# Order of the last attention group's softmax and of layer 2's first products, and of the loads of the later x groups, in a four-layer graph network kernel

## The chip, the cores and the metric

The kernel runs on one core of one Trainium2 chip. The metric is the device time of one execution in microseconds (us). The core has TensorE (PE, with its weight loads as PEld), VectorE (DVE), ScalarE (ACT), GpSimd (POOL) and SyncE (SP, which here only issues DMAs). Each works through its own queue of instructions in order, and they wait for each other by semaphores.

## The reference, cut to what matters

Four layers are applied to x (128 graphs, 64 nodes, 256 features, float32), each behind a layernorm and a relu and each added to x. The change touches the end of layer 1 and the start of layer 2.

```python
# layer 1: attention over the 64 nodes of a graph, 4 heads of 64
h = jnp.maximum(_layernorm(x), 0.0)
qkv = h @ W                                   # q, k, v
scores = einsum('bhid,bhjd->bhij', q, k) / sqrt(64) + mask   # mask: -inf where adj == 0
x = x + einsum('bhij,bhjd->bhid', softmax(scores), v)
# layer 2: mix over nodes, two linear layers with batchnorm
h = jnp.maximum(_layernorm(x), 0.0)
agg = einsum('nm,bmd->bnd', A_hat, h)
h = relu(batchnorm(agg @ W1.T + b1))          # fc1: 256 -> 512
x = x + batchnorm(h @ W2.T + b2)
```

Layer 0 (before) is a graph convolution followed by LSTMs over windows of nodes; layer 3 (after) is three graph convolutions.

## The kernel before

The 8192 tokens are cut into 16 groups of 512 (`NG = 16`), held as tiles `xs[0]` to `xs[15]` in SBUF. `NK = 4` groups make a quarter. The first four x tiles live from the start. The other twelve lie in memory that the LSTM stage has used; right after that stage one loop allocates them and issues all twelve loads (`load_x`, 512 KB each, on SP's queue).

Layer 1 is a loop over groups with a software pipeline. In iteration g, for group g: `values` (v = h times the weights, L779) in two halves, `queries_keys` (q and k by seven products of half-size blocks, L757, with ACT copies p at L171 and L172), `to_residual` (adds the LSTM's result to x four groups ahead, where there is one), `features` (the transposed h of the next group, ACT copies `hT` at L263, DVE differences at L196 to L200), and `softmax` (scores L803, mask L810, row maximum L817, subtraction L818, exp L819). For group g - 1: the row sums (`sums_of`, L824), `turn` (transposes of exp, L835, and copies eT), `attend` (exp times v, L848). For group g - 2: `add_output` (L860 on DVE divides by the row sums, L863 on POOL adds to x). The layernorm of group g + 2 (statistics L92 to L98 on DVE with a power on POOL, L96, and four ACT instructions, L111) stands after the subtraction.

Each half of `values` is copied from PSUM to one staging tile, `vt` (L784, a single buffer), and four DMAs on SP's queue (L787) regroup it into v. A next copy into `vt` waits until the four have landed.

Layer 2 begins inside the last iterations. `activated` is the layernorm and relu of a group, `mixed` its product with the adjacency (L143, copies at L155), `hidden` the products of fc1 (four of them, L729) and, for each, the batchnorm statistics (L735, DVE) and the bias on ACT (L736). In iteration 15 group 0 is mixed, group 1's layernorm is issued, then attend of group 14 and the scores and softmax of group 15. A seventeenth pass of the loop (g = 16) then does two products of group 0's fc1, group 1's mix, `add_output` of group 14, the turn of group 15, the other two products, attend of group 15 and its `add_output`. A loop over the groups 1 to 15 follows: layernorm and mix of group g + 1, all four products of group g.

The order in which the instructions stand on each engine is made by a scheduler from the program's order, its own estimates, and hints: `tc.issue_after(i)` lets nothing in its block stand ahead of instruction i. PSUM has eight banks, given out by `bank()`.

Of the kernel before, what the change touches and what calls it, by code (L numbers as in the profile page):

```python
# [8 lines left out]
F32 = mybir.dt.float32  # L9
# [29 lines left out]
def adj_preln_kernel(ctx: ExitStack, tc: tile.TileContext, x_in, adj, vec, bg0, bg1,  # L39
# [17 lines left out]
    def load_x(x, g):  # L57
        nc.sync.dma_start(out=x, in_=x_view[:, g * GT : (g + 1) * GT, :])
# [639 lines left out]
    xpool_b = ctx.enter_context(tc.tile_pool(name="xres_b", bufs=1, reuse_waits="tile"))  # L698
    for g in range(NK, NG):
        xs.append(xpool_b.tile([P, GT, D], F32, tag=f"x{g}", name=f"x{g}"))  # L700
        load_x(xs[g], g)


    def arena(pool):
# [14 lines left out]
    def mixed(g, copies):  # L719
        h = h1s[g][:, 0:2, :].rearrange("p a (b d) -> p (a b) d", d=D)  # L720
        return mix(h, ah2, 2, h1s[g][:, 2:4, :], copies)

    def hidden(g, w1, ms=range(4)):
        a = h1s[g]
        pss, counted = [], []
        for m in ms:
            ps = bank()
            for c in range(2):
                nc.tensor.matmul(  # L729
                    ps, lhsT=w1[:, c, m * P : (m + 1) * P], rhs=a[:, 2 + c, :],  # L730
                    start=(c == 0), stop=(c == 1),
                )
            pss.append(ps)
        for m, ps in zip(ms, pss):
            counted.append(nc.vector.bn_stats(st1[:, m, g, :], ps))  # L735
            nc.scalar.activation(  # L736
                a[:, m, :], ps, AF.Identity, bias=vecs[:, V_B1 + m : V_B1 + m + 1]
            )
        return counted


    with tc.tile_pool(name="att", bufs=2, reuse_waits="tile") as ap_:
# [28 lines left out]
        def values(hT, v, ks):  # L771


            for k in ks:
                ps = bank((P, 2, D))
                for t in range(2):
                    tok = (2 * k + t) * P
                    for c in range(2):
                        nc.tensor.matmul(  # L779
                            ps[:, t, :], lhsT=hT[:, c, tok : tok + P], rhs=wv[:, c, :],  # L780
                            start=(c == 0), stop=(c == 1),
                        )
                vt = ap_.tile([P, 2, D], F32, tag="vt", name="vt", bufs=1)
                nc.scalar.copy(vt, ps)  # L784
                for par in range(2):
                    for b in range(2):
                        nc.sync.dma_start(  # L787
                            out=v[par * 64 : par * 64 + 64, 4 * k + b : 4 * k + 4 : 2, :],
                            in_=vt[b * 64 : b * 64 + 64, :, par * P : (par + 1) * P],
                        )  # L790

        def softmax(qT, kT):


            e = ap_.tile([P, 2 * GT, 2, NODES], F32, tag="e", name="e")
            pss = [bank((P, 2 * GT, NODES)) for _ in range(2)]
            for t in range(GT):
                for m in range(2):
                    for b in range(2):
                        tok = t * P + b * NODES  # L800
                        for par in range(2):
                            rows = slice(par * 64, par * 64 + 64)
                            nc.tensor.matmul(  # L803
                                pss[par][b * 64 : b * 64 + 64, 2 * t + m, :],
                                lhsT=qT[rows, m, tok : tok + NODES],
                                rhs=kT[rows, m, tok : tok + NODES],
                                start=True, stop=True,
                            )
            for par in range(2):
                nc.vector.scalar_tensor_tensor(  # L810
                    e[:, :, par, :], pss[par], 0.125,
                    mask.unsqueeze(1).to_broadcast([P, 2 * GT, NODES]), ALU.mult, ALU.add,
                )
            ef = e.rearrange("p a q j -> p (a q) j")
            NH = 4 * GT
            mx = ap_.tile([P, NH, 1], F32, tag="mx", name="mx")
            nc.vector.tensor_reduce(mx[:, :, 0], ef, AX.X, ALU.max)  # L817
            sub = nc.vector.tensor_tensor(ef, ef, mx.to_broadcast([P, NH, NODES]), ALU.subtract)  # L818
            nc.scalar.activation(ef, ef, AF.Exp)  # L819
            ri = ap_.tile([P, 2 * GT, 2, 1], F32, tag="ri", name="ri")  # L820
            rif = ri.rearrange("p a q o -> p (a q o)")

            def sums_of():
                nc.vector.tensor_reduce(rif, ef, AX.X, ALU.add)  # L824
                nc.vector.reciprocal(rif, rif)

            return e, ri, sub.ins, sums_of

        def turn(e):

# [25 lines left out]
        def add_output(g, pss, ri):  # L856
            xv = xs[g].rearrange("p t (m q d) -> p (t m) q d", m=2, q=2)
            for par in range(2):
                o = ap_.tile([P, 2 * GT, NODES], F32, tag="o", name="o")
                nc.vector.tensor_tensor(  # L860
                    o, pss[par], ri[:, :, par, :].to_broadcast([P, 2 * GT, NODES]), ALU.mult
                )
                nc.gpsimd.tensor_tensor(out=xv[:, :, par, :], in0=xv[:, :, par, :], in1=o, op=ALU.add)  # L863

# [4 lines left out]
        nc.vector.tensor_tensor(wsum, wqk[0][1], ss[1], ALU.subtract)  # L871
        wqk_blocks = (*wqk, ss + [wdiff, wsum])
        last = None
        for g in range(NG + 1):
            if g == NG - NK + 1:
                hres_pool.__exit__(None, None, None)
                with tc.using_default_side("right"):
                    ar_right = ctx.enter_context(
                        tc.tile_pool(name="arena_r", bufs=NG // 2, reuse_waits="tile")
                    )  # L880
            if g == NG:

                hidden(0, w1, range(2))
                mixed(1, (on_scalar, on_scalar))
            if g < NG:
                hT_all, blocks = hT
                v = ap_.tile([P, 2 * GT, P], F32, tag="v", name="v")
                values(hT_all, v, (0,))
                q, k, finish = queries_keys(blocks)
                if g == 0:  # L890
                    h = normalized(1)
            if last is not None:
                with tc.issue_after(finish.behind):
                    if g > 1:
                        add_output(g - 2, pss, ri)
                    sums_of()
            if last is not None:
                e, ri, v_last = last
                eT, turned = turn(e)
            if g < NG:  # L900
                added = finish()
                if g == NG - 1:

                    w1 = w_att[:, :, 0:512]
                    w2 = w_att[:, :, 512:1024].rearrange("p a (b f) -> a p b f", f=D)
                    nc.sync.dma_start(out=w1, in_=w1t.rearrange("(c p) f -> p c f", p=P))
                values(hT_all, v, (1,))
            else:
                counted = hidden(0, w1, range(2, 4))
            if 0 < g <= NG - NK:  # L910
                to_residual(g + NK - 1, xs[g + NK - 1], ap_, 1)
            if g + 1 < NG:
                hT = features(transposed(h))
            if g == NG - 1:
                with tc.issue_after(mixed(0, (on_scalar, on_scalar))), tc.issue_after(added):
                    activated(ar_right, 1)
            if last is not None:
                pss = attend(eT, v_last)
            if g < NG:
                e, ri_next, sub, sums_of = softmax(q, k)  # L920
                last = (e, ri_next, v)
                with tc.issue_after(sub):
                    if g + 2 < NG:
                        h = normalized(g + 2)
                    elif g + 2 == NG:
                        activated(ar_right, 0)
            else:
                add_output(g - 1, pss, ri)
                after_attention = sub


    ar_left = ctx.enter_context(tc.tile_pool(name="arena_l", bufs=NG // 2 - 1, reuse_waits="tile"))
# [23 lines left out]

    behind = [[], [], counted]
    for g in range(1, NG):
        if g + 1 < NG:
            with tc.issue_after(behind[g - 1][-1].ins if behind[g - 1] else after_attention):  # L960
                pool = ar_right if g + 1 < NG // 2 else keep if g + 1 == NG // 2 else ar_left
                activated(pool, g + 1, (lambda: behind[g][1]) if behind[g] else None)
                mixed(g + 1, (on_scalar, on_vector))
        if g == 3:
            for a in range(2):
                nc.sync.dma_start(
                    out=w2[a], in_=w2t.rearrange("(a b p) f -> a p b f", a=2, p=P)[a]
                )
        behind.append(hidden(g, w1))
# [336 lines left out]
```

## Time and profile before

| | us |
|---|---|
| median of 3 runs (2499.6 to 2501.5) | 2500.47 |
| profiled execution, its own time | 2501.49 |
| its span | 2499.7 |
| PE busy / DVE busy / ACT busy / POOL busy | 2458.1 / 1514.5 / 1145.4 / 439.0 |
| mean granted PE clock | 0.993 |
| attention loop: mask of group 0 to the end of the last attend | 1232.3 to 1472.6 |

A line of the timeline gives the start in us from the span's start, the length in us, the engine, the line of the kernel, the operation, what it writes and reads, how many instructions are merged, and in brackets the engine's idle time ahead of it with what ended it. A line of the table of windows gives the stretch, the busy us of PE, PEld, DVE, ACT and POOL with the number of instructions, the mean granted PE clock (1.00 is full), the busy share of the DMA engines, and GB/s. A float32 matmul shows as two passes.

### The profile page before, as it was taken

The page shows a single profiled execution, that of the slowest core. Times are in us where ns is not written, and L with a number is a line of the kernel's source. Part 1 is how long each engine was busy: PE and PEld are TensorE (multiplying, and loading weights), DVE is VectorE, ACT ScalarE, POOL GpSimd, SP SyncE. Part 2 cuts the span into 40 slices and gives each one's busy share as a digit, 9 for nine tenths or more (in the row PEclk, how much of TensorE's full clock was granted, in tenths as well). Part 3 has the DMA queues.
Part 4 walks back from the last instruction along what each step waited for, and adds up shares of the span by engine and source line. Part 5 has one row for each costly group of instructions (what it writes and reads, how often), then busy time and mean ns, then how long its engine had stood idle before and what let it go on. Part 6 is the DMA issues. An engine that isn't in the chain of part 4 may idle for free.

```text
span 2499.7 us, 46255 instructions
## 1 busy us (share of the span) xinstructions
PE 2458.1 (98%) x19614; PEld 2075.3 (83%) x19614; DVE 1514.5 (61%) x2716; ACT 1145.4 (46%) x2027; POOL 439.0 (18%) x368
## 2 busy tenths in 40 slices
PE   8999999999999999999999999998999999999999
PEld 5668888889999998888888854446898898888888
DVE  6658876656566565566599976425556454454544
ACT  4547754444354353444456566753333333333332
POOL 4422211111111111111133321003111111101110
PEclk9999999999999999999999999998999999999999
DMA  3200000001000000000311110010000000000000
GB/s 114 103 2 1 1 17 1 1 1 34 1 1 1 1 1 1 1 13 1 110 44 38 37 31 1 1 59 1 10 9 18 10 10 10 18 10 10 18 9 18
DMA packets 48526, 48.00 MB, mean 19 GB/s; under 512 B 3648, under 2 KB 44736, under 8 KB 48320
## 3 DMA queue, kind: packets, MB, share of 16 engines
q1 hardware_dynamic: 47616, 44.49, 5.8%
q8 instruction: 154, 2.52, 0.4%
q10 hardware_dynamic: 704, 0.56, 0.1%
q14 instruction: 52, 0.43, 0.1%
HBM read 28.26 MB, written 8.39 MB: 15 GB/s over the span
## 4 chain that ended last, share of the span: by engine, by line
PE 87%; DVE 6%; ACT 3%; issue 1%; POOL 1%; DMA 1%; SPq 0%; DVEq 0%; ACTq 0%; POOLq 0%
PE ps L505 40%; PE ps L1120 15%; PE ps L1165 8%; PE ps L729 4%; PE ps L1012 4%; PE ps L143 3%; PE ps L1084 3%; PE ps L427 2%; PE ps L451 2%; PE ps L757 2%; PE ps L779 1%; ACT arena L217 1%; POOL arena L178 1%; DMA v<-vt 1%; DMA x<-in_x 1%
## 5 line engine op out<-in xcount | busy, mean ns | idle before, releaser
L1120 PE MATMUL ps<-arena 128*128 128x256 f32 x1792 | 392.9, 381 | 1.6 <-DVE arena L198 1.6
L505 PE MATMUL ps<-diff,s 128*128 128x256 f32 (+1 forms) x1824 | 393.5, 371 | 0.9 <-DVE diff L621 0.9
L1120 PEld LDWEIGHTS ps<-arena 128*128 128x128 f32 x1792 | 337.8, 190 | 56.1 <-issue 10.3
L505 PEld LDWEIGHTS ps<-diff,s 128*128 128x128 f32 x1824 | 345.9, 190 | 33.8 <-issue 1.6
L519 ACT ACTIVATE gates<-gates,lbias 128x512 f32<-128x512 f32 (+5 forms) x426 | 244.2, 621 | 202.3 <-DVE gates L183 146.7
L178 POOL TENSOR_TENSOR gates<-p 128x512 f32<-128x512 f32 (+1 forms) x115 | 149.3, 1299 | 882.0 <-DVE p L175 831.0
L505 PE MATMUL ps<-h,w 128*128 128x256 f32 (+1 forms) x1028 | 241.2, 371 | 1.6 <-ACT p L171 1.6
L505 PE MATMUL ps<-diff,w 128*128 128x256 f32 (+1 forms) x1040 | 238.7, 370 | 0.0
L505 PEld LDWEIGHTS ps<-diff,w 128*128 128x128 f32 x1040 | 197.4, 190 | 18.2
L505 PEld LDWEIGHTS ps<-h,w 128*128 128x128 f32 x1028 | 194.6, 190 | 20.9 <-ACT p L171 2.0
L519 ACT ACTIVATE gates<-ps,lbias 128x256 f32<-128x256 f32 (+3 forms) x213 | 91.8, 477 | 247.3 <-PE ps L505 247.1
L217 ACT ACTIVATE arena<-arena 128x512 f32<-128x512 f32 (+1 forms) x160 | 88.5, 582 | 192.7 <-POOL arena L178 103.3
L178 POOL TENSOR_TENSOR arena<-arena 128x512 f32<-128x512 f32 x64 | 72.9, 1139 | 535.9 <-DVE arena L175 535.9
L1165 PE MATMUL ps<-arena 128*128 128x128 f32 x1280 | 149.9, 276 | 0.0
L183 DVE TENSOR_TENSOR gates<-p,ps 128x512 f32<-128x512 f32 (+1 forms) x115 | 76.3, 664 | 120.2 <-PE ps L505 120.2
L1165 PEld LDWEIGHTS ps<-arena 128*128 128x128 f32 x1280 | 145.6, 192 | 1.3 <-issue 0.2
L96 POOL TENSOR_TENSOR rstd<-rstd,mhalf 128x4 f32<-128x4 f32 (+1 forms) x66 | 66.5, 1007 | 423.5 <-DVE rstd L95 421.0
L183 DVE TENSOR_TENSOR arena<-arena,ps 128x512 f32<-128x512 f32 x64 | 39.7, 621 | 149.5 <-PE ps L1120 84.7
L174 DVE TENSOR_TENSOR p<-p,ps 128x512 f32<-128x512 f32 (+1 forms) x131 | 86.7, 661 | 51.3 <-PE ps L505 51.2
L505 PE MATMUL ps<-state,w 128*128 128x256 f32 (+1 forms) x512 | 116.1, 370 | 0.9 <-ACT p L171 0.8
L729 PE MATMUL ps<-arena,w 128*128 128x512 f32 x256 | 116.1, 607 | 0.0
L505 PE MATMUL ps<-state,s 128*128 128x256 f32 (+1 forms) x512 | 115.8, 369 | 0.0
(203 smaller groups left out, 4033.0 us busy)
## 6 DMA issues: line engine op xcount, KB each, us to landing
x<-in_x SPq DMA_DIRECT2D x27, 512.0 KB, 7.3
v<-vt SPq DMA_DIRECT2D x128, 64.0 KB, 2.1
out<-x SPq DMA_DIRECT2D x15, 512.0 KB, 2.9
w<-in_wih SPq DMA_DIRECT2D x4, 1024.0 KB, 7.4
w<-in_whh SPq DMA_DIRECT2D x3, 1024.0 KB, 6.2
arena<-in_l3w SPq DMA_DIRECT2D x3, 1024.0 KB, 5.1
w<-in_wqkv SPq DMA_DIRECT2D x1, 768.0 KB, 4.7
x<-in_x SPq DMA_DIRECT2D x2, 256.0 KB, 3.0
```

The costliest lines, as they stand in the source:

```text
L143: nc.tensor.matmul(pss[b][half * 64 : half * 64 + 64, c, t, :], lhsT=src[rows, t, col : col + 64], rhs=a2[rows, :], start=True, stop=True,)
L174: nc.vector.tensor_tensor(p1, p1, ps[2], ALU.add)
L178: nc.gpsimd.tensor_tensor(out=out[1][1], in0=p1, in1=p5, op=ALU.add)
L183: nc.vector.tensor_tensor(out[0][1], p1, ps[1], ALU.add)
L217: nc.scalar.activation(o, o, func)
L505: nc.tensor.matmul(ps[:, r], lhsT=wc[:, j, :], rhs=bc, start=first and r == 0 and c == 0, stop=True, skip_group_check=True,)
L519: nc.scalar.activation(o, ps, func, bias=lbias[:, col : col + 1])
L729: nc.tensor.matmul(ps, lhsT=w1[:, c, m * P : (m + 1) * P], rhs=a[:, 2 + c, :], start=(c == 0), stop=(c == 1),)
L1012: nc.tensor.matmul(pss[m], lhsT=w2[c // 2][:, c % 2, m * P : (m + 1) * P], rhs=a[:, c, :], start=(c == 0), stop=(c == 3),)
L1084: nc.tensor.matmul(ps[:, t, :], lhsT=w[:, t * P : (t + 1) * P], rhs=b, start=first and t == 0, stop=True, skip_group_check=True,)
L1120: nc.tensor.matmul(ps[:, r, :], lhsT=w[:, c, col : col + P], rhs=b[:, c, :], start=first and r == 0 and c == 0, stop=c == 1, skip_group_ch ...
L1165: nc.tensor.matmul(ps[:, t, :], lhsT=w[:, c, t * P : (t + 1) * P], rhs=b[:, c, :], start=first and t == 0 and c == 0, stop=c == 3, skip_gr ...
```

## The change

Three things are edited. The loop over x tiles loads only those of the groups 4 to 7; each iteration g of the attention loop calls `load_x` for group g + 8 after the first half of `values`. The seventeenth pass of the loop is written out behind the loop in another order. `softmax` is split in two: `scores` (products and mask) and the rest; for the last group the mask is placed inside group 1's layernorm, and `add_output` of group 14 inside group 2's layernorm, which now begins there. `hidden` is split into its products and its evictions, and group 0's second half and group 1's first half of fc1 stand around the turn of group 15.

```diff
     for g in range(NK, NG):
         xs.append(xpool_b.tile([P, GT, D], F32, tag=f"x{g}", name=f"x{g}"))
-        load_x(xs[g], g)
+        if g < 2 * NK:
+            load_x(xs[g], g)
...
     def hidden(g, w1, ms=range(4)):
+        return hidden_out(g, ms, hidden_products(g, w1, ms))
+
+    def hidden_products(g, w1, ms):
...
+    def hidden_out(g, ms, pss):
...
-        def softmax(qT, kT):
+        def scores(qT, kT):
...
+            return e, masked
+
+        def softmax(e):
...
-        for g in range(NG + 1):
+        for g in range(NG):
...
-            if g == NG:
-
-                hidden(0, w1, range(2))
-                mixed(1, (on_scalar, on_scalar))
...
+            values(hT_all, v, (0,))
+            if g + 2 * NK < NG:
+                load_x(xs[g + 2 * NK], g + 2 * NK)
+            q, k, finish = queries_keys(blocks)
...
             if g == NG - 1:
-                with tc.issue_after(mixed(0, (on_scalar, on_scalar))), tc.issue_after(added):
-                    activated(ar_right, 1)
+                turned_in = mixed(0, (on_scalar, on_scalar))
             if last is not None:
                 pss = attend(eT, v_last)
...
+            if g < NG - 1:
+                masked_scores()
             else:
-                add_output(g - 1, pss, ri)
-                after_attention = sub
+                with tc.issue_after(turned_in), tc.issue_after(added):
+                    activated(ar_right, 1, masked_scores)
+            ri_next, sub, sums_of = softmax(e_next[0])
...
+        e, ri_next, v_last = last
+        with tc.issue_after(sub):
+            counted = hidden(0, w1, range(2))
+            mixed(1, (on_scalar, on_scalar))
+            pss_0 = hidden_products(0, w1, range(2, 4))
+            h1s.append(arena(ar_right))
+            rstd, nmr, _ = ln_scale(xs[2], lambda: add_output(NG - 2, pss, ri))
+        eT, turned = turn(e)
+        with tc.issue_after(turned):
+            ln_apply(xs[2], h1s[2][:, 0:2, :].rearrange("p a (b d) -> p (a b) d", d=D), rstd, nmr)
+            counted += hidden_out(0, range(2, 4), pss_0)
+        sums_of()
+        counted_next = hidden(1, w1, range(2))
+        pss = attend(eT, v_last)
+        add_output(NG - 1, pss, ri_next)
+        after_attention = sub
...
     for g in range(1, NG):
+        if g == 1:
+            mixed(2, (on_scalar, on_vector))
+            behind.append(counted_next + hidden(1, w1, range(2, 4)))
+            continue
```

More of the change, by code (lines that the diff above doesn't have):

```diff
@@ L723, in hidden @@
     def hidden(g, w1, ms=range(4)):
+        return hidden_out(g, ms, hidden_products(g, w1, ms))
+    def hidden_products(g, w1, ms):
         a = h1s[g]
-        pss, counted = [], []
+        pss = []
         for m in ms:
@@ L733, in hidden @@
             pss.append(ps)
+        return pss
+    def hidden_out(g, ms, pss):
+        a = h1s[g]
+        counted = []
         for m, ps in zip(ms, pss):
@@ L809, in softmax @@
             for par in range(2):
-                nc.vector.scalar_tensor_tensor(
+                masked = nc.vector.scalar_tensor_tensor(
                     e[:, :, par, :], pss[par], 0.125,
@@ L825, in sums_of @@
                 nc.vector.reciprocal(rif, rif)
-            return e, ri, sub.ins, sums_of
+            return ri, sub.ins, sums_of
         def turn(e):
@@ L859, in add_output @@
                 o = ap_.tile([P, 2 * GT, NODES], F32, tag="o", name="o")
-                nc.vector.tensor_tensor(
+                last = nc.vector.tensor_tensor(
                     o, pss[par], ri[:, :, par, :].to_broadcast([P, 2 * GT, NODES]), ALU.mult
@@ L863, in add_output @@
                 nc.gpsimd.tensor_tensor(out=xv[:, :, par, :], in0=xv[:, :, par, :], in1=o, op=ALU.add)
+            return last
         wsum = ap_.tile([P, D], F32, tag="wsum", name="wsum", bufs=1)
@@ L880, in adj_preln_kernel @@
                     )
-            if g == NG:
-                hidden(0, w1, range(2))
-                mixed(1, (on_scalar, on_scalar))
[L885 to L891, printed above, removed]
+            hT_all, blocks = hT
+            v = ap_.tile([P, 2 * GT, P], F32, tag="v", name="v")
+            values(hT_all, v, (0,))
+            if g + 2 * NK < NG:
+                load_x(xs[g + 2 * NK], g + 2 * NK)
+            q, k, finish = queries_keys(blocks)
+            if g == 0:
+                h = normalized(1)
             if last is not None:
@@ L899, in adj_preln_kernel @@
                 eT, turned = turn(e)
[L900 to L909, printed above, removed]
+            added = finish()
+            if g == NG - 1:
+                w1 = w_att[:, :, 0:512]
+                w2 = w_att[:, :, 512:1024].rearrange("p a (b f) -> a p b f", f=D)
+                nc.sync.dma_start(out=w1, in_=w1t.rearrange("(c p) f -> p c f", p=P))
+            values(hT_all, v, (1,))
             if 0 < g <= NG - NK:
@@ L914, in adj_preln_kernel, with masked_scores @@
             if g == NG - 1:
-                with tc.issue_after(mixed(0, (on_scalar, on_scalar))), tc.issue_after(added):
-                    activated(ar_right, 1)
+                turned_in = mixed(0, (on_scalar, on_scalar))
             if last is not None:
                 pss = attend(eT, v_last)
[L919 to L926, printed above, removed]
-            else:
-                add_output(g - 1, pss, ri)
-                after_attention = sub
+            e_next = []
+            def masked_scores():
+                e, masked = scores(q, k)
+                e_next.append(e)
+                return masked
+            if g < NG - 1:
+                masked_scores()
+            else:
+                with tc.issue_after(turned_in), tc.issue_after(added):
+                    activated(ar_right, 1, masked_scores)
+            ri_next, sub, sums_of = softmax(e_next[0])
+            last = (e_next[0], ri_next, v)
+            with tc.issue_after(sub):
+                if g + 2 < NG:
+                    h = normalized(g + 2)
+                elif g + 2 == NG:
+                    activated(ar_right, 0)
+        e, ri_next, v_last = last
+        with tc.issue_after(sub):
+            counted = hidden(0, w1, range(2))
[12 more added lines that the diff above has]
+        after_attention = sub
     ar_left = ctx.enter_context(tc.tile_pool(name="arena_l", bufs=NG // 2 - 1, reuse_waits="tile"))
```

## The prediction

> Numbers count microseconds (us) from the start of the profiled span. "Group 15" is the last of the 16 token groups; "idle" is idle time of TensorE (PE).
>
> **What bounds the kernel now.** First the page's busy times:
>
> ```profile
> PE 2458.1 (98%) x19614; PEld 2075.3 (83%) x19614; DVE 1514.5 (61%) x2716; ACT 1145.4 (46%) x2027; POOL 439.0 (18%) x368
> ```
>
> PE is idle for only 41.6 us, so a change that leaves its work alone can win back only idle time and slow clock. The table of 10 us windows over the attention stage shows where these are:
>
> ```profile
> 1240.00:1250.00 10.00, 7.52 (x131) 6.38 (x134) 5.88 (x11) 6.04 (x11) 1.73 (x2) 0.91 0.24 53
> 1250.00:1260.00 10.00, 10.00 (x80) 8.62 (x73) 8.38 (x18) 4.29 (x8) 2.26 (x2) 0.92 0.22 54
> ...
> 1300.00:1310.00 10.00, 9.86 (x158) 8.64 (x160) 9.43 (x23) 7.29 (x13) 5.93 (x5) 1.00 0.16 38
> ...
> 1460.00:1470.00 10.00, 6.87 (x77) 4.31 (x74) 7.54 (x18) 4.36 (x7) 1.82 (x2) 0.66 0.01 2
> ```
>
> Columns: PE, PEld, DVE, ACT, POOL busy, then PE's granted clock. An ordinary window (1300) has 0.14 us idle; the two places that the change touches have 2.48 and 3.13, and behind both the clock falls. The timeline of the first place:
>
> ```profile
> 1220.04 13.88 SPq L58 DMA_DIRECT2D x<-in_x  x12
> ...
> 1234.02 27.56 SPq L787 DMA_DIRECT2D v<-vt  x20
> ...
> 1244.30 0.69 PE L848 MATMUL ps<-v,eT 64*64 64x64 f32 x32
> ...
> 1246.35 0.33 PE L848 MATMUL ps<-v,eT 64*64 64x64 f32 x2 [1.35 <-DMA v<-vt]
> ...
> 1249.12 2.01 PE L803 MATMUL ps<-k,q 64*64 64x64 f32 x57
> ...
> 1251.06 1.84 PEld L779 LDWEIGHTS ps<-w,hT 128*128 128x128 f32 x8
> ```
>
> Twelve x loads stand on SP's queue ahead of the first values v. Group 0's second half of v is issued at 1244.22, and attend (L848) waits for it; the next scores (L803) then run at half speed. The second place, at the entry to layer 2:
>
> ```profile
> 1459.83 1.16 PE L143 MATMUL ps<-ah,arena 64*64 64x64 f32 x64
> ...
> 1463.01 1.06 ACT L819 ACTIVATE e<-e 128x1024 f32<-128x1024 f32 x1 [0.38 <-DVE e L818]
> ...
> 1464.12 1.97 PE L835 MATMUL ps<-ident,e 128*128 128x128 f32 x8 [3.13 <-ACT e L819]
> ...
> 1465.88 5.68 PE L729 MATMUL ps<-arena,w 128*128 128x512 f32 x8
> ...
> 1474.46 7.13 PE L729 MATMUL ps<-arena,w 128*128 128x512 f32 x16
> ...
> 1482.62 7.13 PE L729 MATMUL ps<-arena,w 128*128 128x512 f32 x16
> ```
>
> PE has nothing to do until group 15's exp is done, then turns it (L835) in 1.97 instead of the 1.09 of other groups, and takes 5.68 for eight passes that later cost 3.53 (half of 7.06, sixteen passes on the chain of waits).
>
> **What the Trainium skill says.** "TensorE: Matmul & The Clock Gate", Part 1: an activity window of about 3.4 us runs free; an idle one drops the array to half clock, a busy one lifts it. The trace agrees in size: clock 0.50 for 3.4 us from 1248.2 and 6.8 us from 1463.2. But a window needn't be all idle here: the two before those drops were a third busy, while the idle 1.17 us at 1427 cost nothing. I take 1.4 us of idle in one window as the limit, an estimate between these. "DMA: Bandwidth & Descriptors", "Queues, rings and completion order": each DMA engine consumes descriptors in ring order. The trace agrees: x loads land 1.5 us apart in order (first 1223.5, twelfth 1240.26) and the first v 0.34 us after the last x. The clock page also has ACT and DVE as strict FIFO, which the argument below uses.
>
> **The x loads.** In the built program they don't go one per iteration: the scheduler puts SP's queue as x4 to x8, v of group 0 first half, x9, x10, second half, x11 to x14, v of group 1 first half, x15, second half. No byte and no instruction is added, and the rest of SP's queue stands as it did. ACT's copies to the single vt buffer move: group 0's second to ahead of the copies p (L171, L172), group 1's first to behind the exp, its second ahead of the hT copies.
>
> Step by step. The first five loads issue from 1220.04 to 1222.67 as before and land by 1229.7. vt is ready at 1225.7 (L784, 1225.12 + 0.57), so v issues 1225.7 to 1228.1 (0.6 each) and lands behind x8, about 1230.5. ACT ends its hT copies at 1231.1 and copies vt (0.57); v second half issues 1231.8 to 1234.2, lands behind x10 by 1236. x11 to x14 issue by 1236.5 and land by 1242.1. Group 1's vt copy follows the exp (1238.2), its v issues 1238.9 to 1241.3, lands about 1243.3. ACT reaches the next vt copy at 1244.8 (eT to 1243.7, hc 1.09); the hT copies end at 1246.5, 0.3 later than before. Attend starts at 1244.3 with all of v landed: 1.09, then scores, and group 2's values (L779) begin at 1246.4, not 1251.06: 4.7 earlier. Then DVE leads: hT differences (4 x 0.42) to 1247.8, mask 1.28, max 1.22, subtract 1.22, exp to 1252.6, while PE arrives at 1251.6: a wait of 1.0. From there to the next mask other groups take 9.85: 1262.5 against 1267.01. **Gain 4.5**. Bounds: 5.3 (three ordinary periods of 14.71 from the mask at 1232.26 end at 1276.4; it was 1281.7), and 2.5, if DVE's lead of 3.2 is what lasts and landings take 0.7 of it. Later loads are needed five iterations after issue, so they cost nothing.
>
> **The last group.** The same PE products in another order: after mix 1, group 0's second half of fc1 (3.53), then the turn, group 1's first half, attend, mix 2, the rest. Nothing changes to 1456.2, the end of scores. DVE: mask 1.28, nmr 0.16, max and subtract 2.44: done 1460.3; ACT: layernorm 1 2.08 to 1460.0, exp to 1461.4, 2.7 earlier. PE: fc1 3.6 and mix 1 1.16 to 1461.0; second half to 1464.5 (its banks are those of the scores, free at 1457.6); turn 1.09 (its banks wait for two bias copies of 0.69 behind the exp, 1462.8: hidden) to 1465.6; fc1 of group 1 to 1469.1; attend and mix 2 1.09 each to 1471.3; other half to 1474.9. Both the idle 3.13 and the one of 0.60 at 1474.07 are covered.
>
> What is late next: DVE and ACT. Layernorm 2 waits on POOL behind the first half of add_output (1.27 + 1.02): nmr 1466.7, ACT to 1468.8, in time for mix 2. Then DVE has statistics 0.69, row sum 1.20, statistics 0.69, reciprocal 0.24, layernorm 3's 1.40 + 0.36, statistics 2 x 0.69, and half of layernorm 4's: nmr 3 at 1473.4, ACT to 1476.0; mix 3 ends 1476.2 with 0.2 waited. The copy of mix 2 (L155), which group 2's fc1 needs, now stands on DVE behind layernorm 4 with its POOL trip (nmr 1475.9) and group 15's two output products (1.25): done 1477.9; ACT's half, behind three layernorm slices, 1478.2. So PE idles 2.1 and starts group 2's fc1 at 1478.3, against 1482.62: 4.3 earlier at full clock. In a free-running window 2.1 us of idle passes 1.4 in about 4 of 5 positions (it is split evenly enough in 0.7 of 3.41); then a window at half clock costs 3.41/2 = 1.7. **Gain 2.6**, bounds 4.3 and 0. After that each group is PE-bound (8.15 us, DVE about 6 of 10), so the lead passes to the end.
>
> Sum: 7.1 off the profiled execution's own 2501.5 (span 2499.7 and 1.8 around it) is 2494.4; the median of the runs is 1.0 below that execution: **2493.4**.
>
> **Rivals.**
> - The x loads only move (0.13): group 1's v waits behind x11 to x14 as group 0's did behind twelve, hT is late by as much as attend gains. For it: 2 MB in front; against: ACT has 1.5 us of slack there. 2500.5 - 2.6 = 2497.9.
> - The new idle time is larger (0.13): DVE's rows take longer among POOL's adds, PE idles 4.2 at 1476, and two windows run at half clock (3.4, as at 1463): 4.3 - 2.1 - 3.4 = -1.2, so 2500.5 - 4.5 + 1.2 = 2497.2. For it: DVE and POOL are in series twice there.
> - Slower (0.07): the vt copy now ahead of p. ACT is in order; before, group 0's second copy stood behind eT, and a landing at 1241.4 hurt little. If the first v lands after 1233.7, p (1234.4) is late one for one, and so are PE's products. Landing at 1241.4 again: 7.6 + 1.7 to 3.4 of clock, against 2.6 gained at the end: about 2507.5. Against it: landings in ring order give 1230.5, 3.2 us of margin.
>
> **How the numbers follow.** The likeliest case has 0.67, with 2490 to 2495.5 as its own range (both upper bounds give 2490.9; clock and landings the rest). The 8-in-10 range runs from 2490.0 to 2499.0 and takes in the first two rivals. A measurement of this kernel tells about 0.2%, 5 us, from no change: the first case is faster by more than that, the two middle ones (0.26) are not, the last is slower.
>
> **What would show it.** Right: in 1240 to 1250 PE near 9.8 busy with clock 1.00; no "DMA v<-vt" wait of attend in the first groups; group 15's exp starting near 1455.8 (1460.3 less the 4.5 won before it), with no wait of the turn for it; in place of the 3.13, a wait of about 2 at group 2's fc1, on the copy L155, with at most one slow window behind it. Wrong: p copies waiting for v in the first iterations, or clock 0.50 for two windows after layer 2's entry.

## The result, and the profile after

| | before | after |
|---|---|---|
| median of 22 executions each, us | 2500.51 | 2496.36 |
| lowest and highest, us | 2497.66 to 2503.29 | 2493.62 to 2498.33 |
| profiled execution, own time / span, us | 2501.49 / 2499.7 | 2495.02 / 2493.2 |

The ratio of the times is 0.9983, with a 95% interval of 0.9976 to 0.9989: 4.15 us (0.17%) faster. The forecast was 2493.4, within 2490.0 to 2499.0. The time lies in that range, 3.0 us above the forecast and above the likeliest case's own upper end (2495.5). The gain is real, but lies just inside the band of 0.2% that the text had called hard to tell from no change; the likeliest case had it outside.

The two profiled executions differ by 6.5 us and not by 4.15, since one was 1.0 above its median and the other 1.3 below. Single times of one kernel spread over 4 to 6 us, so the stages below are compared inside the traces, and the totals by medians.

The busy time of PE in the profile after (compare 2458.1):

```profile
PE 2454.6 (98%) x19614; PEld 2073.4 (83%) x19614; DVE 1516.3 (61%) x2716; ACT 1145.8 (46%) x2027; POOL 439.3 (18%) x368
```

As many instructions, and PE is 3.5 us less busy: less of its work runs at the slow clock. The other 3.0 us of the span's 6.5 are idle time less. The table of windows after (columns as before: PE, PEld, DVE, ACT, POOL busy, then PE's granted clock):

```profile
1240.00:1250.00 10.00, 8.11 (x162) 7.00 (x161) 6.20 (x13) 5.68 (x10) 1.51 (x2) 0.93 0.79 220
1250.00:1260.00 10.00, 10.00 (x46) 8.47 (x45) 9.39 (x19) 6.07 (x11) 3.89 (x4) 0.90 0.15 36
...
1460.00:1470.00 10.00, 10.00 (x154) 5.78 (x153) 8.30 (x26) 6.01 (x12) 3.55 (x4) 1.00 0.01 2
1470.00:1480.00 10.00, 8.07 (x80) 3.92 (x79) 8.41 (x28) 7.25 (x14) 5.41 (x5) 1.00 0.01 2
```

At layer 2's entry the hole at 1460 (6.87 busy, clock 0.66) is full; a smaller one stands at 1470, as forecast, and no slow clock behind it in this execution. But 1240, forecast at 9.8 with clock 1.00, has 8.11 and 0.93: the first place still has a hole. The timeline of PE there:

```profile
1243.69 1.16 PE L861 MATMUL ps<-v,eT 64*64 64x64 f32 x64
1244.68 1.11 PE L812 MATMUL ps<-k,q 64*64 64x64 f32 x64
1247.68 2.96 PE L788 MATMUL ps<-w,hT 128*128 128x256 f32 x8 [1.89 <-ACT hT L263]
1250.42 3.58 PE L766 MATMUL ps<-hT,w 128*128 128x256 f32 x12
```

Lines have moved: attend was L848 and is L861, the values were L779 and are L788. Attend no longer waits for v, and the scores behind it run at full speed. In its place the next values wait 1.89 for hT, and they and q/k behind them take 2.96 and 3.58 instead of 1.99 and 2.75. The timelines of SP's queue and of ACT tell why:

```profile
1225.39 2.64 SPq L796 DMA_DIRECT2D v<-vt  x4
1228.07 1.17 SPq L58 DMA_DIRECT2D x<-in_x  x2
1232.74 2.82 SPq L796 DMA_DIRECT2D v<-vt  x4
1235.61 2.29 SPq L58 DMA_DIRECT2D x<-in_x  x4
1238.35 2.71 SPq L796 DMA_DIRECT2D v<-vt  x4
```

```profile
1246.55 0.59 ACT L793 COPY vt<-ps 128x512 f32<-128x512 f32 x1 [2.07 <-DMA v<-vt]
1247.03 1.08 ACT L263 COPY hT<-ps 128x512 f32<-128x512 f32 x2
```

Group 1's first half of v (issued 1238.35) stands behind the four loads x11 to x14. Until it has landed, the one vt buffer is in use; ACT waits 2.07 for it, and the hT copies stand behind on the same engine. Layer 2's entry, from the timeline of all engines:

```profile
1462.03 1.04 PE L848 MATMUL ps<-ident,e 128*128 128x128 f32 x8
...
1472.09 1.86 PE L143 MATMUL ps<-ah,arena 64*64 64x64 f32 x64
...
1474.79 0.68 DVE L155 COPY arena<-ps 128x512 f32<-128x512 f32 x1
1475.20 0.56 ACT L155 COPY arena<-ps 128x512 f32<-128x512 f32 x1
...
1475.82 7.13 PE L733 MATMUL ps<-arena,w 128*128 128x512 f32 x16 [1.87 <-ACT arena L155]
```

The turn waits for nothing and takes 1.04 instead of 1.97. The forecast wait on mix 2's copies is there, 1.87.

Two distances inside each trace serve below: **A**, from group 0's values to layer 2's first mix (before 1219.84 to 1453.22: 233.38; after 1219.52 to 1450.79: 231.27), and **B**, from there to group 2's fc1 (before 29.40; after 25.03). The profile after thus runs 0.32 ahead of the one before when the attention stage begins. A is a coarse measure: its later part alone, from group 3's values to the first mix, takes from 186.4 (after) to 188.0 (e6) in the profiles below, with moved loads (e1 187.9) and without (before 187.0, e2 187.9).

### The profile page after: what moved, and what is told of

It is laid out like the page before. It is cut to its first block, busy times and chain, and to the rows that moved or that the text cites. A ratio compares the mean times of both kernels' runs of the same rounds, so it can differ in the third digit from the quotient of the medians.

```text
span 2493.2 us, 46254 instructions
## 1 busy us (share of the span) xinstructions
PE 2454.6 (98%) x19614; PEld 2073.4 (83%) x19614; DVE 1516.3 (61%) x2716; ACT 1145.8 (46%) x2027; POOL 439.3 (18%) x368
## 4 chain that ended last, share of the span: by engine, by line
PE 87%; DVE 7%; ACT 2%; issue 1%; POOL 1%; DMA 1%; SPq 0%; DVEq 0%; ACTq 0%; POOLq 0%
PE ps L505 40%; PE ps L1157 15%; PE ps L1202 8%; PE ps L1049 4%; PE ps L733 4%; PE ps L143 3%; PE ps L1121 3%; PE ps L451 2%; PE ps L427 2%; PE ps L766 2%; PE ps L788 1%; ACT arena L217 1%; DVE st L92 1%; POOL arena L178 1%; DVE e L831 0%
```

## The experiments

"Gain" is the median of the kernel before, in the same series, less the kernel's own. A and B are from one profile each.

| run | median us | gain us | ratio to before, 95% interval | A | B |
|---|---|---|---|---|---|
| the change | 2496.36 | 4.15 | 0.9983 [0.9976, 0.9989] | 231.27 | 25.03 |
| e1_x_only | 2498.72 | 2.2 | 0.9992 [0.9983, 1.0] | 233.57 | 27.54 |
| e2_last_only | 2497.89 | 3.05 | 0.9989 [0.9982, 0.9995] | 234.68 | 24.87 |
| e3_vt2 | 2493.01 | 7.9 | 0.9968 [0.9956, 0.9981] | 229.77 | 25.05 |
| e4_spread | 2493.85 | 7.1 | 0.9973 [0.9962, 0.9983] | 229.94 | 24.86 |
| e5_copy2 | 2493.64 | 6.8 | 0.9974 [0.9965, 0.9984] | 232.02 | 23.90 |
| e6_exp_only | 2496.50 | 3.95 | 0.9985 [0.9978, 0.9992] | 234.12 | 25.07 |
| e7_vt2_copy2 | 2491.58 | 8.9 | 0.9964 [0.9951, 0.9977] | 229.73 | 24.10 |
| e8_vt2_spread_copy2 | 2491.97 | 8.5 | 0.9964 [0.9951, 0.9977] | 229.56 | 24.10 |
| e9_before_vt2 | 2497.63 | 3.2 | 0.9987 [0.998, 0.9993] | 231.23 | 28.52 |
| e10_vt2_copies_apart | 2490.73 | 10.1 | 0.9961 [0.9947, 0.9974] | 229.35 | 23.63 |

The theory after the result: the last group's part gains what the sum said, and the x loads' part only half, because the single vt buffer passes the landing of v on to ACT's queue and so to hT. The rival: DVE's lead, and not hT, takes the other half.

### Each part alone

e1, on the kernel before:

```diff
-        load_x(xs[g], g)
+        if g < 2 * NK:
+            load_x(xs[g], g)
...
                 values(hT_all, v, (0,))
+                if g + 2 * NK < NG:
+                    load_x(xs[g + 2 * NK], g + 2 * NK)
```

> The kernel before with the x loads' edit alone. Marker: the first mix of layer 2 (L143), which starts at 1453.22 in the profile before and at 1450.79 after the whole change. Reading of the trace after (theory): the edit alone is worth about 2.1 us, since group 1's first half of v still lands behind x11 to x14 and holds ACT's next vt copy and hT: L143 near 1451, a PE wait near 1.9 on ACT's hT copies with a slow window behind it, time near 2498.4. As predicted: 4.5 us, no such wait, L143 near 1448.7, 2496.0. Rival, loads only move: no gain, L143 near 1453.2, 2500.5.

e2, on the changed kernel, undoes the same lines.

> The changed kernel with all x loads up front again, so the last group's part alone. Theory: 4.4 us at full clock from layer 2's first mix to group 2's fc1, less 0 to 1.7 us by whether a half-clock window follows the wait of 1.9 us: time 2496.1 to 2497.8; group 2's fc1 29.4 us minus 4.4 = 25.0 us behind the first mix. Rival, the gain of the two parts isn't additive and the last group alone gives the whole 4.1: 2496.4 with e1 at 2500.5. The old wait of attend on v of 1.35 us and the slow window at 1248 are back.

The gains are 2.2 and 3.05, beside 4.5 and 2.6 in the prediction. Their sum, 5.25, and the 4.15 of both together agree within the intervals. The interval of e1 reaches to no change (ratio 1.0), so its 2.2 is likely but not shown. Its time is the theory's, but its first mix stood at 1453.45, where the rival had it, and not near 1451. In part its profile caught a still longer wait on hT. The timeline of PE in e1:

```profile
1249.35 3.42 PE L780 MATMUL ps<-w,hT 128*128 128x256 f32 x8 [3.19 <-ACT hT L263]
```

From group 0's values to group 3's, the stretch that holds the old wait and the new one, e1 took 45.6, the change 44.8 and the kernel before 46.4. That is 0.8 of the 2.3 between e1 and the change in A; the other 1.5 come later, where A differs without the loads too.

So the wait is not one number. Across the five profiles with moved loads and one vt buffer it is 1.89 (after), 3.19 (e1), 2.43 (e5), 2.88 (e6) and, with the loads spread, none (e4); A of the first four lies between 231.3 and 234.1. In e2 the timeline of PE shows the other end as expected, with the same wait and no slow window behind it:

```profile
1479.88 7.13 PE L732 MATMUL ps<-arena,w 128*128 128x512 f32 x16 [1.85 <-ACT arena L155]
```

### What holds hT: the buffer or the loads

e3, on the changed kernel (mx gives up a buffer for room; it is used by DVE alone):

```diff
-                vt = ap_.tile([P, 2, D], F32, tag="vt", name="vt", bufs=1)
+                vt = ap_.tile([P, 2, D], F32, tag="vt", name="vt", bufs=2)
...
-            mx = ap_.tile([P, NH, 1], F32, tag="mx", name="mx")
+            mx = ap_.tile([P, NH, 1], F32, tag="mx", name="mx", bufs=1)
```

> The changed kernel with two vt buffers in place of one (mx has one in place of two, for room). Theory, the single vt buffer behind x11 to x14 is what holds hT: ACT's vt copy of group 1's second half starts at 1244.5 instead of 1246.55, PE's wait of 1.89 at group 2's values goes or falls to 0.3, and so does the slow window behind it; layer 2's first mix 2 to 2.4 us earlier than after (near 1448.6), time near 2494.2. Rival, DVE's lead of 3.2 us is what sets the pace there: the wait goes but comes back at the mask and the turn, layer 2's first mix within 0.5 of 1450.8, time 2496.4. Rival, ACT itself is late (hT after its own queue): the wait stays near 1.9.

e4, on the changed kernel; `values` returns its last DMA:

```diff
-            if g + 2 * NK < NG:
-                load_x(xs[g + 2 * NK], g + 2 * NK)
...
-            values(hT_all, v, (1,))
+            moved = values(hT_all, v, (1,))
+            if g + 2 * NK < NG:
+                with tc.issue_after(moved.ins):
+                    load_x(xs[g + 2 * NK], g + 2 * NK)
```

> The changed kernel with the later x loads held behind the second half of v of their iteration on SP's queue, so that they really go one per iteration. Theory: v(1,0) has one load of 512 KB ahead of it in place of four and lands near 1241.5, before ACT wants vt; the wait of 1.89 goes as in e3, layer 2's first mix near 1448.6, time near 2494.2. Rival, DVE sets the pace: first mix within 0.5 of 1450.8, time 2496.4. Rival, a late x: a wait of PE or DVE on an x load in groups 3 to 11, time over 2497.

Both times came near the theories' 2494.2: 2493.01 and 2493.85, 3.4 and 2.5 us under the change. A fell to 229.8 and 229.9, by 1.5 and 1.3, where the theories had the first mix 2 to 2.4 earlier. The timeline of PE in e3:

```profile
1246.14 1.99 PE L788 MATMUL ps<-w,hT 128*128 128x256 f32 x8
...
1252.30 1.09 PE L848 MATMUL ps<-ident,e 128*128 128x128 f32 x8 [0.71 <-ACT e L832]
...
1474.75 8.83 PE L733 MATMUL ps<-arena,w 128*128 128x512 f32 x16 [1.86 <-ACT arena L155]
```

The values start without a wait, and group 1's turn stands at 1252.30 with 0.71 waited: the prediction had 1252.6 with 1.0. So DVE's lead takes back 0.71 of the 1.89, not all of it; that rival falls.

But e3 changes more than the buffer. ACT can copy group 0's second half earlier, and with it group 1's first half of v now goes ahead of the four loads. The timeline of SP's queue in e3:

```profile
1234.79 2.61 SPq L796 DMA_DIRECT2D v<-vt  x4
1237.44 3.49 SPq L58 DMA_DIRECT2D x<-in_x  x4
```

Both runs thus took the four loads from in front of that v, e4 with one buffer and e3 with two, and in both the wait on hT at group 2's values is gone. That the loads in front of v cause it is shown; whether a second buffer alone would end it, with the four loads still in front, was not run. e9 below shows what the buffer does by itself in the kernel before.

In e3's timeline of PE the last line shows the half-clock window that the change's own profile missed: 8.83 instead of 7.13, 1.70 for the 1.7 of the sum. e4 has it too (8.79). In e4 smaller waits come one group earlier, by its timeline of PE:

```profile
1232.62 2.05 PE L788 MATMUL ps<-w,hT 128*128 128x256 f32 x8 [0.49 <-ACT hT L263]
...
1240.62 1.09 PE L849 MATMUL ps<-ident,e 128*128 128x128 f32 x8 [1.20 <-ACT e L833]
```

There ACT's vt copies wait for landings of group 0's v, the first for 0.79 ahead of hT, the second, for 3.58 until 1236.63, ahead of p and the exp: the mechanism of the prediction's slower rival, at 1.20 us of price.

e9 puts the two vt buffers into the kernel before, with no load moved (the edit of e3); SP's queue has all twelve loads and then v, as before.

> The kernel before, all twelve x loads still in front, with two vt buffers (mx with one). Theory, what the loads cost is paid through the single vt buffer: v's second half of group 0 is issued right behind the first (about 1238.2 to 1240.7), lands near 1242.5, before attend (1244.3); the waits of 1.35 and 0.92 and the slow window go without a load being moved, layer 2's first mix stands 229.7 to 230.5 us behind group 0's values (233.38 before), time 2496 to 2497.5. Rival, the loads in front of the first v are the cost: attend still waits for v by 1 us or more, 2499.5 or more.

The gain is 3.2, A 231.23. The timeline of PE in e9:

```profile
1245.05 0.62 PE L848 MATMUL ps<-v,eT 64*64 64x64 f32 x25 [0.17 <-DMA v<-vt]
...
1247.22 2.05 PE L779 MATMUL ps<-w,hT 128*128 128x256 f32 x8 [0.56 <-ACT hT L263]
...
1461.96 1.09 PE L835 MATMUL ps<-ident,e 128*128 128x128 f32 x8 [3.48 <-ACT e L819]
```

Attend's waits of 1.35 and 0.92 shrink to 0.17 although the twelve loads still stand in front: ACT copies group 0's second half at 1228.86 instead of 1243.61. The expectation's A of 229.7 to 230.5 was missed by 0.7 and its time by 0.1; the landings held ACT for 0.69 and 0.51 once more and hT was 0.56 late. (The last line is the old wait at layer 2's entry, which this edit leaves.) A second buffer alone gained 3.2 and moving the loads alone 2.2; their intervals overlap, so which is better isn't settled. Together, with the last group's part, they gain 7.9.

### The last group: which half of the edit, and the new wait

e6, on the changed kernel, takes the fc1 products back from beside the exp chain:

```diff
             mixed(1, (on_scalar, on_scalar))
-            pss_0 = hidden_products(0, w1, range(2, 4))
...
-            counted += hidden_out(0, range(2, 4), pss_0)
+            counted += hidden(0, w1, range(2, 4))
         sums_of()
-        counted_next = hidden(1, w1, range(2))
...
-            behind.append(counted_next + hidden(1, w1, range(2, 4)))
+            behind.append(hidden(1, w1))
```

> The changed kernel with group 15's exp chain still ahead of layernorm 1 and the outputs, but group 0's second half of fc1 behind the turn and group 1's first half behind mix 2 again, as before the change. Theory A, the exp chain carries the gain: PE waits 0.4 for exp at the turn and about 2.3 for layernorm 2 at mix 2, but loses no more than 0.5 to the changed kernel: group 2's fc1 25.0 to 25.6 us behind layer 2's first mix, time 2496.4 to 2497. Theory B, the fc1 beside it carries half of the 4.4: group 2's fc1 27 us behind the first mix, time 2498.5.

2496.50, and B is 25.07 against 25.03: theory A, though the wait at mix 2 is 0.88 and not 2.3. The timeline of PE in e6:

```profile
1462.20 1.09 PE L848 MATMUL ps<-ident,e 128*128 128x128 f32 x8 [0.25 <-ACT e L832]
...
1468.70 1.94 PE L143 MATMUL ps<-ah,arena 64*64 64x64 f32 x64 [0.88 <-ACT arena L111]
...
1479.24 7.13 PE L733 MATMUL ps<-arena,w 128*128 128x512 f32 x16
```

With the exp early, the turn waits only 0.25. The fc1 products that the change puts beside it fill that and the 0.88 at mix 2, and then the same time is waited for at group 2's fc1: its copy comes when DVE and ACT are through with the layernorms. Bringing PE's work forward gained nothing where the other engines set the date.

e5, on the changed kernel:

```diff
-            mixed(2, (on_scalar, on_vector))
+            copied_2 = mixed(2, (on_scalar, on_scalar))
...
-            with tc.issue_after(behind[g - 1][-1].ins if behind[g - 1] else after_attention):
+            with tc.issue_after(behind[g - 1][-1].ins if behind[g - 1] else after_attention), tc.issue_after(copied_2):
```

> The changed kernel with both copies of mix 2 (L155) on ACT, ahead of layernorm 3 and 4 there, instead of one on DVE behind group 15's output products and one on ACT behind the layernorm slices. Theory: PE's wait of 1.87 at group 2's fc1 goes (mix 3 ends 1473.95, fc1 follows by 1474.1 on the scale of the profile after, 23.2 us behind layer 2's first mix instead of 25.03), and with it the half-clock window that some executions have there; the x loads' wait of 1.9 in group 1 stays. 1.8 us less 0 to 1.7: time 2493.0 to 2494.6. Rival, another release ends next (mix 3 on layernorm 3, now behind the copies on ACT, or fc1's banks): at most 0.5 us, 2496.

2493.64, 2.7 us under the change. B is 23.90, not 23.2. The timeline of PE in e5:

```profile
1474.80 1.92 PE L143 MATMUL ps<-ah,arena 64*64 64x64 f32 x64 [0.68 <-ACT arena L111]
1476.65 7.13 PE L733 MATMUL ps<-arena,w 128*128 128x512 f32 x16
```

The 1.87 goes, and 0.68 comes back at mix 3: the two copies put layernorm 3 back on ACT, as the rival had it. B accounts for 1.1 of the 2.7; the rest fits a slow window that is now missing in executions that had it, but no profile of e5 against one of the change shows that difference, and single values spread by more.

e7 has the edits of e3 and e5; e8 that of e4 besides.

> The two vt buffers of e3 and the copies of e5 together. Theory, the two waits stand in different places and their gains add: e3's 2493.0 less e5's gain of 1.8 to 3.5: 2489.5 to 2491.2. Rival, the lead of one is taken back by the other: 2492.5 or more.

> As e7, with e4's loads besides, one per iteration behind the second half of v. Theory, with two vt buffers no copy of ACT waits for a landing any more, so it matters little where the loads stand: within 0.7 of e7. Rival, the loads in front of v delay it still, through attend: 1 us or more faster than e7.

e7 took 2491.58, 1.4 under e3 and just outside the expected 2489.5 to 2491.2: mix 3's wait on layernorm 3 is 0.88 there. Five times each don't separate e7 (2490.61 to 2493.78) from e3 (2491.94 to 2493.94), so that the two gains add is likely, not shown. e8 is within 0.4 of e7: with two buffers, whether the later loads go in the scheduler's order or one per iteration makes no difference that these runs can show. All twelve in front still cost something, as e9 against e3 shows from group 0's values to group 3's (44.0 and 42.5).

e10, on e7, puts one copy on each engine again, each ahead of what it stood behind (`kept` also notes the copy in `copies_2`):

```diff
+        copies_2 = []
...
+        mixed(2, (kept(on_scalar), kept(on_vector)))
+        with tc.issue_after(copies_2[1].ins):
+            add_output(NG - 1, pss, ri_next)
-        add_output(NG - 1, pss, ri_next)
...
-            mixed(2, (on_scalar, on_vector))
...
-            with tc.issue_after(behind[g - 1][-1].ins if behind[g - 1] else after_attention):
+            with tc.issue_after(behind[g - 1][-1].ins if behind[g - 1] else after_attention), tc.issue_after(copies_2[0].ins):
```

> As e7 (two vt buffers), but mix 2's copies one on ACT, ahead of layernorm 3, and one on DVE, ahead of group 15's output products. Theory: layernorm 3 on ACT is no longer put back by two copies, so mix 3's wait of 0.88 goes; DVE's copy ends near 1474.2 on the scale of the profile after, so fc1 of group 2 waits about 0.3: 23.5 us behind layer 2's first mix (24.10 in e7, 25.05 in e3), time 2491.0. Rival, what e7 gained came from the copies' place alone and mix 3 is bound by layernorm 3 anyway: as e7, 2491.6.

2490.73, for 2491.0 expected and 2491.6 by the rival; B is 23.63. The timeline of PE in e10:

```profile
1470.71 1.93 PE L143 MATMUL ps<-ah,arena 64*64 64x64 f32 x64 [0.40 <-ACT arena L111]
1472.57 7.13 PE L733 MATMUL ps<-arena,w 128*128 128x512 f32 x16
```

Of 1.87 at fc1 and nothing at mix 3, 0.40 at mix 3 is left. B is 0.47 shorter than in e7; the five times of each overlap. This version beats both kernels: 10.1 us under the one before, with all its five times (2490.16 to 2491.96) below the lowest of the change (2493.62).

## Why the prediction was right or wrong

- **The order of SP's queue** was right. Group 0's v landed later than forecast, but within the margin: its first half by 1232.06 (1230.5), its second by 1237.04 (1236). ACT's copy of the second half waited 1.36 for the first, until 1232.13; attend ran at 1243.69 without a wait.
- **The x loads' gain of 4.5 was mis-sized: 2.2 in e1's median, with an interval down to 0.0, and 2.1 in A of the change's profile.** The step that failed is "x11 to x14 issue by 1236.5 and land by 1242.1 ... its v ... lands about 1243.3. ACT reaches the next vt copy at 1244.8". ACT was there at 1244.48, as said. But a transfer completes in 16 parts (the 16 updates of its semaphore in the trace), and the prediction's landings are those of the first part: its 1223.5 for the first x load is one, and the last part came at 1224.11. A copy that waits needs the last. This told twice:
  - Group 0's first half of v had its last transfer's first part at 1230.52 and its last at 1232.06. That held ACT's copy, so the second half was issued until 1235.56, not 1234.2 (issuing also took 0.4 longer), and x11 to x14 from 1235.61. The first part of x14 came at 1243.97 instead of 1242.1, and that of group 1's v at 1245.19 instead of 1243.3.
  - From that first part to the last it took another 1.26. ACT's copy began at 1246.55, 0.10 behind it.

  So hT was 1.6 later than in the sum, 1.9 with the 0.32 by which this profile is ahead; PE waited 1.89, and a half-clock window followed. Group 2's mask stood at 1264.46 instead of 1262.5 (before 1267.01).
- **The first rival named this mechanism** ("hT is late by as much as attend gains") and gave it 0.13. The argument against it, 1.5 us of slack on ACT, was used up by the landing. It came true in part: attend's waits of 1.35 and 0.92 went, and 1.89 on hT came. The time lies in the stated range because that range took in the rivals; the likeliest case, at 0.67, ended at 2495.5.
- **The rest of that part fits e3**, which has group 1's first half of v ahead of the loads and two buffers: with the wait gone, the values start at 1246.14 (1246.4), the turn waits 0.71 (1.0), and the whole gains 7.9 with an interval of 4.8 to 11, for 7.1 forecast.
- **The last group's part was right in its mechanism, and its size close with some luck**: 4.3 at full clock forecast, 29.40 - 25.03 = 4.37 in the trace; group 15's exp starts 7.06 behind the first mix (1457.85), as in the sum; the wait on the copy 2.1 forecast, 1.87 measured; the window behind it 1.7 forecast, 1.70 in e3. Its share was said to be 4 of 5; of the four profiles that have the wait (after, e2, e3, e4), two show it. The net of 2.6 compares with 3.05 in e2, whose interval is 1.3 to 4.5.
- **What the forecast didn't see there**: the 29.40 of before itself holds two half-clock windows, and they come and go. With the same instruction order there and one such window, e1 has 27.54 and e9 28.52, so against them the change's 25.03 is 2.5 and 3.5 shorter, not 4.37. And the fc1 products beside the exp chain, counted as cover for 3.13 and 0.60, were not needed: e6 gains the same without them.
- **The other rivals** fell: no second slow window at 1476, and in the changed kernel no p copy waiting for v (the vt copy ended at 1232.72, p came at 1234.08).

## What to carry to other kernels

Ask of every moved transfer which buffer it holds until it lands, which engine refills that buffer, and what stands behind the refill in that engine's queue; a single buffer between an engine and a DMA turns late bytes into a late engine. Where a stage is late on two engines, bring forward what the last one waits for: moving the bound engine's own work forward only moves its wait. And count a landing by the last of a transfer's completions, not by the first.

## What the runs showed of the hardware

- **The 16 completions of one DMA can lie far apart.** A 64 KB transfer of v with no load under way completed within 0.25 us (1250.97 to 1251.22 in the profile after). Behind x11 to x14 the spread was 1.26 there and 2.31 in e1 (1245.81 to 1248.12); behind the twelve loads it was 1.9 in the profile before (1241.42 to 1243.36) and up to 3.2 in e9. The copies that waited began about 0.1 behind the last one. "DMA: Bandwidth & Descriptors", "Queues, rings and completion order" in the Trainium skill, gives ring order for each engine, not one order for all of them; the runs agree. What sets the spread stays open, and loads in front aren't all of it: in e4 a v transfer issued at 1232.73, after the last load in front had landed at 1229.63, was spread over 1.30.
- **An idle time of 1.9 to 2.9 us brings a half-clock window in some executions and not in others.** 1.85 in e2 and 2.43 in e5 had none behind them; 1.86 in e3, 1.89 in the profile after and 2.88 in e6 had one. That fits the free-running window which "TensorE: Matmul & The Clock Gate", Part 1, in the Trainium skill describes, and makes a single profile a poor measure of a change of 2 us. The page has the clock fall after an idle window; here PE was still busy for 1.52 of the 3.41 us ahead of the fall in the profile after, and for 1.49 in e3.
